# Layer 1: the q and k projections as seven block products each in place of eight, and a PSUM ring of single-bank tiles

## The chip, the cores and the metric

The kernel runs on one core of a Trainium2 chip. The metric is the device time of the whole program in microseconds (us), from launch to end, as the median of several executions. A profiled execution, taken by the hardware profiler, gives the start and length of every instruction; its span runs from the first to the last instruction.

Engines in the profile: PE is the matrix engine (TensorE), with its weight loads listed apart as PEld; DVE is VectorE, ACT is ScalarE, POOL is GpSimd and SP is SyncE, which issues the DMAs here. "L1745" is line 1745 of the kernel.

## The reference, cut to what matters

The input `x` has 128 rows (s) of 256 positions with 256 channels, all in fp32. Two layers follow one another, each with a group normalization, an attention along the 256 positions and a residual. Layer 0 attends with 8 heads, a pair bias and a gate. The change concerns layer 1, a banded attention with 4 heads of 64 channels:

```python
qkv = x2 @ w_in.T + b_in
q, k, v = jnp.split(qkv, 3, axis=-1)
...
scores = jnp.einsum('bhid,bhjd->bhij', q, k) / jnp.sqrt(jnp.asarray(D, x.dtype))
keep = jnp.abs(i - j) <= band          # band = 16
scores = jnp.where(keep, scores, -jnp.inf)
attn = jax.nn.softmax(scores, axis=-1)
out = jnp.einsum('bhij,bhjd->bhid', attn, v)
y = out @ w_out.T + b_out
...
x = x + _L1_conv_ref(_gn(x), L1_conv_w_in, L1_conv_b_in, L1_conv_w_out, L1_conv_b_out, 16)
```

For each row, q and k are the products of a 256 x 256 weight with a 256 x 256 block of activations.

## The kernel before

**Layer 0** fills about two thirds of the time (up to about 2090 us of the span). The change doesn't touch it. A third kernel part, `general_kernel`, runs only if a check at the end finds values out of range, and doesn't run here.

**Layer 1** works on pairs of rows: 64 pairs (`NP`), each an object of class `Pair1`. Activations are kept transposed: `xgT` is [128 partitions, 2 channel halves k, 512], where the 512 columns are the 256 positions of row r = 0 followed by those of row r = 1. The methods of a pair are:

- `turn` (DVE, L1730) transposes the loaded rows; `centre(k)` (ACT, L1735) subtracts the mean, and after k = 1 has POOL add the output bias to the residual (L1737).
- `project("qT" or "kT", m)` (L1745): for each output half m, two matmuls over k, 128 x 128 by 128 x 512, accumulate in one PSUM bank of the ring `ps_mm` (two banks). ACT adds the bias and writes to `qT` or `kT` (L1749).
- `values(r)` (L1760): the v projection of one row, evicted by ACT (L1764).
- `scores(r)` (L1774): small matmuls of 64 x 64 by 64 x 96 into the two banks of `ps_s`; one exponential of both banks on ACT (L1782), and the band mask on POOL (L1784).
- `apply(r)` (L1802): the weighted values into two banks `o_eo` and the softmax sums into `su_eo`, each for odd and even key blocks.
- `combine(r)`: ACT copies the odd sums and outputs (L1812, L1813), DVE adds the even sums (L1814), inverts (L1815), adds the even outputs (L1816) and multiplies (L1818) into `oT`. For the last eight pairs DVE also checks the range of the inverses here (`check`, L958 to L960).
- `out_row(r)` (L1833): the output projection into a bank of `ps_mm`; DVE adds the residual (L1837).

An fp32 `matmul` call shows in the trace as two weight loads and two matmuls, so a pair's projections (8 calls) are 16 matmuls.

The order on each engine is written out by hand in a loop over p with 63 rounds (`manual_schedule`). Three pairs are in flight in a round: `was` (p - 1), `now` (p) and `nxt` (p + 1), with `nn` being prepared. In the first half of a round: `now.scores(0)`, `was.apply(1)`, `was.out_row(0)`, `was.combine(1)`, three of the four projections of `nxt`, `nn.centre(0)`. In the second half: `now.scores(1)`, `now.apply(0)`, `now.combine(0)`, the fourth projection, `nxt.values` for both rows, `was.out_row(1)`, `nn.centre(1)`, `n3.turn()` and, in some rounds, one deferred range check on DVE. An engine takes its instructions in this order, and waits at one whose operands or buffers are not ready.

[...]

Of the kernel before, what the change touches and what calls it, by code (L numbers as in the profile page):

```python
# [21 lines left out]
def bcast(ap, axis, n):  # L22

    ap = ap.unsqueeze(axis)
    shape = list(ap.shape)
    shape[axis] = n
    return ap.broadcast_to(shape)
# [746 lines left out]
def fast_kernel(  # L774
# [889 lines left out]
    rsum1 = dram.tile([NP, H1, 2, I], F32, name="rsum1")  # L1664
    with tc.tile_pool(name="l1", bufs=2) as sb, tc.tile_pool(
        name="l1s", bufs=4
    ) as sm, tc.tile_pool(name="ps1_mm", bufs=2, space=PSUM) as ps_mm, tc.tile_pool(
        name="ps1_s", bufs=1, space=PSUM
    ) as ps_s, tc.tile_pool(name="ps1_o", bufs=1, space=PSUM) as ps_o:

        def mm1(name):
            return ps_mm.tile([P, 512], F32, name=name, tag="mm")

        nM1 = const.tile([P, KC], F32, name="nM1")

        def norm1():

            each = sm.tile([P, 2, C], F32, name="gn_each", bufs=1)
            dev = sm.tile([P, C], F32, name="gn_dev", bufs=1)
            R1c = sm.tile([P, KC], F32, name="gn_R", bufs=1)  # L1680
            ps = ps_s.tile([P, 2, 512], F32, name="ps_gn", tag="s")
            by_group = lambda a: a.rearrange("p (g e) -> p g e", e=GE)
            nc.vector.tensor_copy(by_group(each[:, 0, :]), bcast(st1[:, :, 1], 2, GE))
            nc.tensor.matmul(ps[:, 0, :C], avg, each[:, 0, :], start=True, stop=True)
            nc.vector.tensor_tensor(dev, each[:, 0, :], ps[:, 0, :C], ALU.subtract)
            nc.vector.tensor_mul(dev, dev, dev)
            nc.vector.scalar_tensor_tensor(
                by_group(each[:, 1, :]), bcast(st1[:, :, 2], 2, GE), 1.0 / (S * NB * GE), by_group(dev), ALU.mult, ALU.add
            )
            for n in range(2):  # L1690
                for k in range(KC):
                    nc.tensor.matmul(
                        ps[:, 1, 2 * n + k : 2 * n + k + 1], each[:, n, k * P : (k + 1) * P], avg[:, 0:1],
                        start=True, stop=True,
                    )
            nc.vector.tensor_scalar_add(R1c, ps[:, 1, 2:4], 1e-5)
            nc.gpsimd.tensor_tensor(R1c, R1c, mhalf[:, :KC], ALU.pow)
            nc.vector.tensor_scalar_mul(nM1, ps[:, 1, 0:2], -1.0)
            for n in range(3):
                for k in range(KC):  # L1700
                    at = slice(n * C, (n + 1) * C)
                    nc.vector.tensor_scalar_mul(w_in[:, k, at], w_in[:, k, at], R1c[:, k : k + 1])


        o_eo = [ps_o.tile([P, 2, I], F32, name=f"ps_o1_{n}", tag=f"o{n}") for n in range(2)]
        su_eo = [ps_o.tile([P, I], F32, name=f"ps_su1_{n}", tag=f"su{n}") for n in range(2)]
        for n in range(2):
            nc.vector.memset(o_eo[n], 0.0)
            nc.vector.memset(su_eo[n], 0.0)

        class Pair1:

# [19 lines left out]
            def centre(self, k):  # L1732
                if k == 0:
                    self.xgT = sb.tile([P, KC, N2], F32, name="xgT1", tag="xgT")
                nc.scalar.activation(self.xgT[:, k, :], self.xT[:, k, :], AF.Identity, bias=nM1[:, k : k + 1])  # L1735
                if k == KC - 1:
                    nc.gpsimd.tensor_tensor(self.xt, self.xt, bcast(bout_r, 1, 2 * NB), ALU.add)  # L1737

            def project(self, which, m):
                n = ("qT", "kT").index(which)  # L1740
# [24 lines left out]

            def scores(self, r):

                ps = ps_s.tile([P, 2, 512], F32, name="ps_sc1", tag="s")
                at = lambda q, c, j: ps[:, q, (c * 2 + j) * W : (c * 2 + j + 1) * W]
                for c in range(KC):  # L1770
                    for k in range(NK):
                        for q in range(2):
                            rs = slice(q * D1, (q + 1) * D1)
                            nc.tensor.matmul(  # L1774
                                at(q, c, k // 2)[half(k)],
                                self.kT[rs, c, r * I + k * KB : r * I + (k + 1) * KB],
                                self.qT[rs, c, r * I + q0(k) : r * I + q0(k) + W],
                                start=True, stop=True,
                            )
                e = sm.tile([P, 2, KC, NK // 2 * W], F32, name="e1", tag="e", bufs=3)  # L1780
                ev = e.rearrange("p q c w -> p q (c w)")
                nc.scalar.activation(ev, ps[:, :, : KC * NK // 2 * W], AF.Exp)  # L1782
                for q in range(2):
                    nc.gpsimd.tensor_tensor(  # L1784
                        e[:, q], e[:, q], bcast(bw.rearrange("p b w -> p (b w)"), 1, KC), ALU.mult
                    )
                self.es[r] = e
# [16 lines left out]
                                )  # L1804

            def combine(self, r):

                if r == 0:
                    self.rv = sb.tile([P, 2, I], F32, name="rv1", tag="rv", bufs=3)
                rv = self.rv  # L1810
                odd = sm.tile([P, 3, I], F32, name="odd1", tag="odd", bufs=2)
                nc.scalar.copy(odd[:, 2, :], su_eo[1])  # L1812
                nc.scalar.copy(odd[:, :2, :], o_eo[1])  # L1813
                nc.vector.tensor_tensor(odd[:, 2, :], su_eo[0], odd[:, 2, :], ALU.add)  # L1814
                nc.vector.reciprocal(rv[:, r, :], odd[:, 2, :])  # L1815
                nc.vector.tensor_tensor(odd[:, :2, :], o_eo[0], odd[:, :2, :], ALU.add)  # L1816
                oT = sb.tile([P, 2, I], F32, name="oT1", tag="oT", bufs=3)
                nc.vector.tensor_tensor(oT, odd[:, :2, :], bcast(rv[:, r, :], 1, 2), ALU.mult)  # L1818
                self.oT[r] = oT
                if r == 1 and self.p < NP - LATE:  # L1820
                    nc.sync.dma_start(rsum1[self.p].rearrange("q r i -> q (r i)"), rv[0:P:DH].rearrange("q r i -> q (r i)"))
                elif r == 1 and self.p < NP - 1:
                    check(rv.rearrange("p r i -> p (r i)"), 1e-16, 1e8, sm)
                elif self.p == NP - 1:
                    check(rv[:, r, :], 1e-16, 1e8, sm)

            def out_row(self, r):
                if r == 0:
                    self.yo = sb.tile([P, 2 * NB, C], F32, name="yo", tag="yo")
                ps = mm1("ps_y1")  # L1830
                for b in range(NB):
                    for k in range(KC):
                        nc.tensor.matmul(  # L1833
                            ps[:, b * C : (b + 1) * C], self.oT[r][:, k, b * P : (b + 1) * P], w_out[:, k, :],
                            start=(k == 0), stop=(k == KC - 1),
                        )
                nc.vector.tensor_tensor(  # L1837
                    self.yo[:, r * NB : (r + 1) * NB, :], ps.rearrange("p (b c) -> p b c", b=NB),
                    self.xt[:, r * NB : (r + 1) * NB, :], ALU.add,
                )  # L1840
                s0 = 2 * self.p
                if self.p == NP - 1:
                    nc.sync.dma_start(rows(out, s0 + r, 1), self.yo[:, r * NB : (r + 1) * NB, :])
                elif r == 1:
                    nc.sync.dma_start(rows(out, s0, 2), self.yo)
# [18 lines left out]
        with tc.manual_schedule():  # L1864
# [3 lines left out]
            norm1()  # L1868
            for k in range(KC):
                now.centre(k)  # L1870
            for m in range(KC):
                now.project("qT", m)
                now.project("kT", m)
            for r in range(2):
                now.values(r)
            for k in range(KC):
                nxt.centre(k)
        check_all(eb.rearrange("p h b i -> p (h b i)"), math.exp(-20.0), math.exp(20.0))
        mask_t = sb.tile([S, I], F32, name="mask_all", bufs=1)
        nc.sync.dma_start(mask_t, mask)  # L1880
# [3 lines left out]
        with tc.manual_schedule():  # L1884
            was = Nobody()
            for p in range(NP - 1):
# [6 lines left out]

                now.scores(0)
                was.apply(1)
                was.out_row(0)
                was.combine(1)
                nxt.project("qT", 0)
                nxt.project("kT", 0)
                nxt.project("qT", 1)  # L1900
                nn.centre(0)

                now.scores(1)
                now.apply(0)
                now.combine(0)
                nxt.project("kT", 1)
                if p < NP - 2:
                    nxt.values(0)
                    nxt.values(1)
                was.out_row(1)  # L1910
                nn.centre(1)
                n3.turn()
                if checks and p > 0:
                    checks.pop(0)()
# [88 lines left out]
```

## Time and profile before

| | us |
|---|---|
| median of 3 runs | 3313.72 (3311.55 to 3315.22) |
| the profiled execution, its own time | 3316.03 |
| its span | 3314.3 |
| PE busy in the span | 3157.9 (95%) |
| DVE, POOL, ACT busy | 2121.6, 1962.8, 1452.7 |
| loop of layer 1, 2133.21 to 3280.69: length | 1147.48 |
| PE busy in it | 1147.01 |
| DVE, ACT, POOL busy in it | 672.15, 525.29, 397.41 |

The page lists busy time of each engine, the chain of work that ended last, and the costliest groups of instructions. An engine that is busy in nearly all of a stretch sets its length, as long as its busy time is streaming and not a wait in the middle of an instruction. The mean granted clock of PE is 0.982.

### The profile page before, as it was taken

The page shows a single profiled execution, that of the slowest core. Times are in us where ns is not written, and L with a number is a line of the kernel's source. Part 1 is how long each engine was busy: PE and PEld are TensorE (multiplying, and loading weights), DVE is VectorE, ACT ScalarE, POOL GpSimd, SP SyncE. Part 2 cuts the span into 40 slices and gives each one's busy share as a digit, 9 for nine tenths or more (in the row PEclk, how much of TensorE's full clock was granted, in tenths as well). Part 3 has the DMA queues.
Part 4 walks back from the last instruction along what each step waited for, and adds up shares of the span by engine and source line. Part 5 has one row for each costly group of instructions (what it writes and reads, how often), then busy time and mean ns, then how long its engine had stood idle before and what let it go on. Part 6 is the DMA issues. An engine that isn't in the chain of part 4 may idle for free.

```text
span 3314.3 us, 80768 instructions
## 1 busy us (share of the span) xinstructions
PE 3157.9 (95%) x34656; PEld 1977.2 (60%) x34656; DVE 2121.6 (64%) x3179; ACT 1452.7 (44%) x2121; POOL 1962.8 (59%) x1375
## 2 busy tenths in 40 slices
PE   5389999999999999999999999699999999999998
PEld 3255555555555555555555555466666666666666
DVE  7955666666666666666666666466655555555566
ACT  2264444444444444444444444244444444444443
POOL 2378777777787777787887776233333333333332
PEclk8699999999999999999999999899999999999999
DMA  9951212212221222222122211533333434343431
GB/s 354 375 137 43 75 49 75 75 46 65 72 75 49 75 75 60 64 64 69 49 75 75 75 49 52 104 79 91 85 90 86 92 85 91 85 92 84 92 90 54
DMA packets 464879, 295.92 MB, mean 89 GB/s; under 512 B 312480, under 2 KB 413728, under 8 KB 463360
## 3 DMA queue, kind: packets, MB, share of 16 engines
q1 hardware_dynamic: 459440, 287.76, 31.7%
q8 instruction: 275, 4.51, 0.6%
q10 hardware_dynamic: 5072, 2.90, 0.3%
q14 instruction: 92, 0.75, 0.1%
HBM read 221.85 MB, written 68.75 MB: 88 GB/s over the span
## 4 chain that ended last, share of the span: by engine, by line
PE 91%; DVE 3%; DMA 3%; ACT 1%; POOL 1%; SPq 1%; issue 0%; ACTq 0%; POOLq 0%; DVEq 0%
PE ps_p L1296 21%; PE ps_p L1745 14%; PE ps_sc L1330 8%; PE ps_y L1833 7%; PE ps_ov L1362 7%; PE ps_v L1760 7%; PE ps_y L1417 7%; PE ps_v L1311 6%; PE ps_o L1802 3%; PE ps_su L1370 3%; PE ps_sc L1774 3%; PE ps_x L1274 2%; PE ps_su L1802 1%; DVE st L1178 1%; DVE zst L1103 1%; DMA zt<-in_z_dram 1%
## 5 line engine op out<-in xcount | busy, mean ns | idle before, releaser
L1351 POOL TENSOR_TENSOR eboth<-e 128x512 f32<-128x512 f32 x512 | 640.6, 1273 | 392.9 <-DVE e L1346 389.7
L1346 DVE TENSOR_TENSOR e<-ps_sc,eb 128x1024 f32<-128x1024 f32 x512 | 603.1, 1219 | 307.0 <-ACT ps_sc L1337 306.9
L1337 ACT ACTIVATE ps_sc<-ps_sc 128x1024 f32<-128x1024 f32 x512 | 492.8, 1006 | 509.2 <-PE ps_sc L1330 509.2
L1784 POOL TENSOR_TENSOR e<-e,bw 128x384 f32<-128x384 f32 x256 | 259.5, 1035 | 769.8 <-ACT e L1782 769.8
L1745 PE MATMUL ps_p<-xgT,w_in 128*128 128x512 f32 x1024 | 470.3, 602 | 4.5 <-issue 3.7
L1745 PEld LDWEIGHTS ps_p<-xgT,w_in 128*128 128x128 f32 x1024 | 190.1, 191 | 203.7 <-issue 174.8
L1330 PE MATMUL ps_sc<-qT,kT 32*128 32x256 f32 x4096 | 293.3, 400 | 2.1 <-ACT kT L1300 2.1
L1296 PE MATMUL ps_p<-xnT,wq 128*128 128x512 f32 x512 | 267.3, 634 | 3.5 <-POOL xnT L1283 3.1
L1833 PE MATMUL ps_y<-w_out,oT 128*128 128x256 f32 x1024 | 250.3, 388 | 2.6 <-DVE oT L1818 2.6
L1837 DVE TENSOR_TENSOR yo<-ps_y,xt 128x512 f32<-128x512 f32 x128 | 88.4, 690 | 251.9 <-PE ps_y L1833 149.7
L1362 PE MATMUL ps_ov<-e,v 128*32 128x256 f32 x4096 | 247.7, 382 | 0.0
L1417 PE MATMUL ps_y<-wo,oT 128*128 128x256 f32 x1024 | 242.1, 379 | 2.0 <-POOL oT L1407 1.2
L1417 PEld LDWEIGHTS ps_y<-wo,oT 128*128 128x128 f32 x1024 | 194.3, 190 | 82.5 <-issue 59.3
L1311 PE MATMUL ps_v<-wv,xnT 128*128 128x256 f32 x1024 | 242.2, 379 | 0.0
L1330 PEld LDWEIGHTS ps_sc<-qT,kT 32*128 32x128 f32 x4096 | 184.9, 184 | 94.4 <-issue 83.6
L1296 PE MATMUL ps_p<-xnT,wk 128*128 128x512 f32 x512 | 240.8, 592 | 0.0
L1296 PE MATMUL ps_p<-xgT,wg 128*128 128x512 f32 x512 | 236.8, 605 | 0.0
L1760 PE MATMUL ps_v<-w_in,xgT 128*128 128x256 f32 x1024 | 231.8, 379 | 0.0
L1815 DVE RECIPROCAL rv<-odd 128x256 f32<-128x256 f32 x128 | 224.4, 1753 | 4.4
L1760 PEld LDWEIGHTS ps_v<-w_in,xgT 128*128 128x128 f32 x1024 | 194.4, 190 | 53.5 <-issue 30.1
L1317 DVE TENSOR_TENSOR v<-ps_v,vb_r 128x512 f32<-128x512 f32 x128 | 88.6, 692 | 206.8 <-PE ps_v L1311 206.8
L1311 PEld LDWEIGHTS ps_v<-wv,xnT 128*128 128x128 f32 x1024 | 189.6, 190 | 50.8 <-issue 31.0
(169 smaller groups left out, 4989.9 us busy)
## 6 DMA issues: line engine op xcount, KB each, us to landing
xa<-in_x_dram SPq DMA_DIRECT2D x8, 4096.0 KB
xt<-in_x_dram SPq DMA_DIRECT2D x64, 512.0 KB
x<-xo SPq DMA_DIRECT2D x16, 2048.0 KB
xs<-x SPq DMA_DIRECT2D x256, 128.0 KB
xt<-x SPq DMA_DIRECT2D x64, 512.0 KB
rvb<-rsum SPq DMA_DIRECT2D x252, 128.0 KB
out_dram<-yo SPq DMA_DIRECT2D x63, 512.0 KB
zt<-in_z_dram SPq DMA_DIRECT2D x15, 2048.0 KB
```

The source lines that it names most:

```text
L1296: nc.tensor.matmul(ps, w[:, k, m * P : (m + 1) * P], getattr(self, src)[:, k, :], start=(k == 0), stop=(k == KC - 1),)
L1311: nc.tensor.matmul(self.ps_v[:, b * C : (b + 1) * C], self.xnT[:, k, t * P : (t + 1) * P], wv[:, k, :], start=(k == 0), stop=(k == KC - 1),)
L1330: nc.tensor.matmul(self.pss[q // 2][:, q % 2, b, :], self.kT[rs, c, r * I + b * P : r * I + (b + 1) * P], self.qT[rs, c, r * I : (r + 1) * I],
L1337: nc.scalar.activation(self.pss[a], self.pss[a], AF.Exp)
L1346: nc.vector.tensor_tensor(e, pss[a], eb[:, h : h + 2], ALU.mult)
L1351: nc.gpsimd.tensor_tensor(t, es[a][:, :, 0, :], es[a][:, :, 1, :], ALU.add)
L1362: nc.tensor.matmul(ov[q * D0 : (q + 1) * D0, c, :], self.v[:, r, b, h * D0 : (h + 1) * D0], es[q // 2][:, q % 2, b, :], start=(b == 0), st ...
L1417: nc.tensor.matmul(self.ps_y[:, b * C : (b + 1) * C], self.oT[r][:, k, b * P : (b + 1) * P], wo[:, k, :], start=(k == 0), stop=(k == KC - 1),)
L1745: nc.tensor.matmul(ps, w_in[:, k, n * C + m * P : n * C + (m + 1) * P], self.xgT[:, k, :], start=(k == 0), stop=(k == KC - 1),)
L1760: nc.tensor.matmul(ps[:, b * C : (b + 1) * C], self.xgT[:, k, t * P : (t + 1) * P], w_in[:, k, 2 * C : 3 * C], start=(k == 0), stop=(k == ...
L1784: nc.gpsimd.tensor_tensor(e[:, q], e[:, q], bcast(bw.rearrange("p b w -> p (b w)"), 1, KC), ALU.mult)
L1833: nc.tensor.matmul(ps[:, b * C : (b + 1) * C], self.oT[r][:, k, b * P : (b + 1) * P], w_out[:, k, :], start=(k == 0), stop=(k == KC - 1),)
```

## The change

The 2 x 2 block product of a weight (blocks by k and m) with the activations of a pair (blocks by k and by row r) has eight block products of 128 x 128 by 128 x 256. The change forms it from seven, in a variant of Strassen's form, for q (n = 0) and for k (n = 1):

- `mix_weights` makes four sums of weight blocks (`wst`) once, on POOL. `differences` makes four sums of activation blocks (`dT`, 256 columns each) for each pair, on POOL.
- `product(n, i)` is one block product. Two PSUM tiles hold a matrix: in `x` the products 1, 6, 7 and 4 accumulate one on another, and after each ACT copies the partial sum out (with a bias) before the next may add to it. In `y` product 2, then 5, then 3 are placed; `join(n, i)` on DVE adds a saved partial sum to `y` and writes a block of `qT` or `kT`.
- The rings `ps_mm` and `ps_s` become one ring of four single-bank tiles, used by the scores (two tiles), the products (two for each matrix) and the values (one each). The exponential of `scores` becomes two instructions, one for each tile.
- `out_row` has no ring any more: it writes to the free halves of the two banks that hold the softmax sums (`su_y`).
- `combine` is cut in three (`copy_odd`, `invert`, `weigh`), which the first half of a round places among the products. All products and joins of a pair stand in the first half of a round now; the second half has none.

```diff
-    ) as sm, tc.tile_pool(name="ps1_mm", bufs=2, space=PSUM) as ps_mm, tc.tile_pool(
-        name="ps1_s", bufs=1, space=PSUM
-    ) as ps_s, tc.tile_pool(name="ps1_o", bufs=1, space=PSUM) as ps_o:
+    ) as sm, tc.tile_pool(name="ps1_s", bufs=4, space=PSUM) as ps_s, tc.tile_pool(
+        name="ps1_o", bufs=1, space=PSUM
+    ) as ps_o:
 
         def mm1(name):
-            return ps_mm.tile([P, 512], F32, name=name, tag="mm")
+            return ps_s.tile([P, 512], F32, name=name, tag="s")
 
         nM1 = const.tile([P, KC], F32, name="nM1")
+        wst = sb.tile([P, 4, 2, P], F32, name="wst", bufs=1)
...
+        def mix_weights():
+
+            a = [[w_in[:, k, 0 : 2 * C].rearrange("p (n m c) -> p m n c", n=2, m=KC)[:, m] for k in range(KC)]
+                 for m in range(KC)]
+            s1, s2, s3, s4 = (wst[:, n] for n in range(4))
+            nc.gpsimd.tensor_tensor(s1, a[1][0], a[1][1], ALU.add)
+            nc.gpsimd.tensor_tensor(s2, s1, a[0][0], ALU.subtract)
+            nc.gpsimd.tensor_tensor(s3, a[0][0], a[1][0], ALU.subtract)
+            nc.gpsimd.tensor_tensor(s4, a[0][1], s2, ALU.subtract)
+
         o_eo = [ps_o.tile([P, 2, I], F32, name=f"ps_o1_{n}", tag=f"o{n}") for n in range(2)]
-        su_eo = [ps_o.tile([P, I], F32, name=f"ps_su1_{n}", tag=f"su{n}") for n in range(2)]
+        su_y = ps_o.tile([P, 2, 2, I], F32, name="ps_su_y1", tag="su")
+        su_eo = [su_y[:, n, 0] for n in range(2)]
...
+            def differences(self):
+
+                self.dT = sb.tile([P, 4, I], F32, name="dT1", tag="dT")
+                b = [[self.xgT[:, k, r * I : (r + 1) * I] for r in range(2)] for k in range(KC)]
+                t1, t2, t3, t4 = (self.dT[:, n] for n in range(4))
+                nc.gpsimd.tensor_tensor(t1, b[0][1], b[0][0], ALU.subtract)
+                nc.gpsimd.tensor_tensor(t2, b[1][1], t1, ALU.subtract)
+                nc.gpsimd.tensor_tensor(t3, b[1][1], b[0][1], ALU.subtract)
+                nc.gpsimd.tensor_tensor(t4, b[1][0], t2, ALU.subtract)
...
+            def product(self, n, i):
+
+                if len(self.ps) == n:
+                    self.ps.append([mm1("ps_qk") for _ in range(2)])
+                x, y = (ps[:, :I] for ps in self.ps[n])
...
+                to, lhs, rhs, start = {
+                    1: (x, w(0, 0), b(0, 0), True),
+                    2: (y, w(0, 1), b(1, 0), True),
+                    6: (x, wst[:, 1, n], self.dT[:, 1], False),
+                    5: (y, wst[:, 0, n], self.dT[:, 0], True),
+                    7: (x, wst[:, 2, n], self.dT[:, 2], False),
+                    4: (x, w(1, 1), self.dT[:, 3], False),
+                    3: (y, wst[:, 3, n], b(1, 1), False),
+                }[i]
+                nc.tensor.matmul(to, lhs, rhs, start=start, stop=True, skip_group_check=True)
...
+                if i in (1, 6, 7):
+                    at = (1, 6, 7).index(i)
+                    nc.scalar.activation(u[:, at], x, AF.Identity, bias=bias(at // 2))
+                elif i == 4:
+                    nc.scalar.activation(self.to[n][:, 1, 0:I], x, AF.Identity, bias=bias(1))
+
+            def join(self, n, i):
+                m, r, at = {2: (0, 0, 0), 5: (1, 1, 2), 3: (0, 1, 1)}[i]
+                nc.vector.tensor_tensor(
+                    self.to[n][:, m, r * I : (r + 1) * I], self.ps[n][1][:, :I], self.u[n][:, at], ALU.add
+                )
...
-                nc.scalar.activation(ev, ps[:, :, : KC * NK // 2 * W], AF.Exp)
+                for q in range(2):
+                    nc.scalar.activation(ev[:, q], ps[q][:, : KC * NK // 2 * W], AF.Exp)
...
-                ps = mm1("ps_y1")
+                ps = su_y[:, :, 1]
...
                 now.scores(0)
                 was.apply(1)
+                nxt.begin_fast()
+                nxt.product(0, 1)
+                was.copy_odd(1)
+                nxt.product(1, 1)
+                for n in range(2):
+                    nxt.product(n, 2)
+                    nxt.join(n, 2)
+                was.invert(1)
+                for i in (6, 5, 7):
+                    for n in range(2):
+                        nxt.product(n, i)
+                for n in range(2):
+                    nxt.join(n, 5)
+                was.weigh(1)
                 was.out_row(0)
-                was.combine(1)
-                nxt.project("qT", 0)
-                nxt.project("kT", 0)
-                nxt.project("qT", 1)
+                for n in range(2):
+                    nxt.product(n, 4)
+                    nxt.product(n, 3)
+                    nxt.join(n, 3)
                 nn.centre(0)
 
                 now.scores(1)
                 now.apply(0)
                 now.combine(0)
-                nxt.project("kT", 1)
                 if p < NP - 2:
                     nxt.values(0)
                     nxt.values(1)
                 was.out_row(1)
                 nn.centre(1)
+                nn.differences()
                 n3.turn()
```

## The prediction

> **What bounds the kernel now.** I read the sums over windows first, because the change touches only the loop of layer 1 and a share over the whole span would mix stages; then the timeline of each engine over one round of that loop; then one place where PE really waits, to price a wait. The two halves of one round, busy time by engine:
>
> ```profile
> core 0: us, PE busy (x) PEld busy (x) DVE busy (x) ACT busy (x) POOL busy (x), PEclk, DMA share, GB/s
> 2404.91:2414.10 9.19, 9.19 (x150) 5.57 (x149) 5.85 (x7) 3.05 (x5) 1.96 (x2) 1.00 0.76 173
> 2414.10:2423.30 9.20, 9.20 (x157) 7.08 (x156) 4.32 (x4) 5.34 (x9) 4.28 (x3) 1.00 0.02 4
> ```
>
> PE is busy for all of 18.39 us; DVE, ACT and POOL have 8 to 12 us of slack, the DMA share doesn't bind. So a matmul taken away is time taken away, unless PE begins to wait. PE's own timeline of the round shows the price of each stage:
>
> ```profile
> 2404.91 0.89 PE L1774 MATMUL ps_sc<-qT,kT 64*64 64x96 f32 x32
> 2407.02 1.99 PE L1833 MATMUL ps_y<-w_out,oT 128*128 128x256 f32 x8
> 2408.85 5.31 PE L1745 MATMUL ps_p<-xgT,w_in 128*128 128x512 f32 x12
> 2414.10 0.89 PE L1774 MATMUL ps_sc<-qT,kT 64*64 64x96 f32 x32
> 2416.21 1.98 PE L1745 MATMUL ps_p<-xgT,w_in 128*128 128x512 f32 x4
> 2418.03 3.62 PE L1760 MATMUL ps_v<-w_in,xgT 128*128 128x256 f32 x16
> 2421.48 1.89 PE L1833 MATMUL ps_y<-w_out,oT 128*128 128x256 f32 x8
> ```
>
> From start to start, 16 matmuls of 256 columns take 2421.48 - 2418.03 = 3.45 us, 0.2156 each, with a new weight load each time. In the weight loads of the projection the step is 0.429 for 512 columns:
>
> ```profile
> 2409.28 0.19 PEld L1745 LDWEIGHTS ps_p<-xgT,w_in 128*128 128x128 f32 x1 [0.24 <-issue]
> 2409.71 0.19 PEld L1745 LDWEIGHTS ps_p<-xgT,w_in 128*128 128x128 f32 x1 [0.24 <-issue]
> ```
>
> A single 256-column matmul lasts 0.379 (the rows of L1760), so a reader on ACT or DVE can start 0.42 after the last pass of a product starts: ACT begins at 2410.77, 0.04 after the modelled end (2410.14 + 0.59) of the projection that it evicts.
>
> **What the Trainium skill says.** "TensorE: Matmul & The Clock Gate", section "LDWEIGHTS (loading the stationary operand)": a load takes columns / 1.2 ns, 107 for 128. The trace agrees in the place where PE waits (below): the second load starts 0.11 us after the first. "PSUM — Partial Sum Buffer", section "PSUM bank collisions raise a hardware error": engines must be kept apart by bank, not by address, so a product may not enter a bank that ACT or DVE still reads; the trace before has no bank that is read and then added to, so the chain of products 1, 6, 7, 4 is new. Its section "The four PSUM rules" allows a synchronised read of a partial sum amid an accumulation; no run shows it yet. "SBUF — State Buffer", section "Who interferes with whom": a DVE instruction with one SBUF input doesn't contend with POOL, one with two does. The trace agrees: L1816 (PSUM and SBUF) takes 0.63 at 2418.85 beside POOL's L1737, while L1818 (two SBUF inputs) right after it takes 1.59 in place of 0.69.
>
> **The change, part by part.** Times t count from the first matmul of a round (2404.91).
>
> Removed: 16 matmuls x 0.429 = 6.864. Added: 14 products x 2 passes x 0.2156 = 6.037. Net -0.83 a round, x 63 rounds = -52 us. The switches between 64-row and 128-row matmuls stay four a round.
>
> The wait that ends this. The place where PE waits in before:
>
> ```profile
> 1842.96 2.50 POOL L1283 TENSOR_TENSOR xnT<-xgT,rs_r 128x512 f32<-128x512 f32 x2 [0.55 <-DMA rs_r<-rs_d]
> 1844.29 2.35 PE L1296 MATMUL ps_p<-xnT,wq 128*128 128x512 f32 x4 [0.34 <-POOL xnT L1283]
> 1844.29 0.30 PEld L1296 LDWEIGHTS ps_p<-xnT,wq 128*128 128x128 f32 x2 [0.74 <-POOL xnT L1283]
> ```
>
> The first POOL multiply ends at 1844.24; the load starts 0.05 later; the loads stand 0.11 apart, so columns stream 0.16 after the releaser's end. A release that comes before the preceding matmul starts costs nothing, since the load runs under it.
>
> Now ACT and DVE in the first half:
>
> ```profile
> 2405.95 0.81 ACT L1782 ACTIVATE e<-ps_sc 128x768 f32<-128x768 f32 x1 [1.45 <-PE ps_sc L1774]
> 2407.16 0.37 ACT L1812 COPY odd<-ps_su 128x256 f32<-128x256 f32 x1 [0.40 <-PE ps_su L1802]
> 2407.43 0.59 ACT L1813 COPY odd<-ps_o 128x512 f32<-128x512 f32 x1
> 2409.72 0.41 DVE L1814 TENSOR_TENSOR odd<-ps_su,odd 128x256 f32<-128x256 f32 x1
> 2410.17 1.75 DVE L1815 RECIPROCAL rv<-odd 128x256 f32<-128x256 f32 x1
> 2411.84 0.63 DVE L1816 TENSOR_TENSOR odd<-ps_o,odd 128x512 f32<-128x512 f32 x1
> ```
>
> Starts show that the engines overlap neighbours: ACT steps 0.27 for the 256 copy, 0.49 for the 512 copy (2421.68 to 2422.17 after L1764), and 0.59 for a biased 512 eviction of 0.69 (2414.20 to 2414.79). Less 0.22 for 256 columns (L1813's 0.59 less L1812's 0.37), my estimate for a biased 256 eviction is a step of 0.37 and a length of 0.47. For a join I take L1814: 0.42, step 0.34.
>
> Product (0,1) streams at 2.22, where the output row streamed, its second pass at 2.43. ACT: eviction from 2.43 + 0.42 = 2.85, then the two copies of `copy_odd` from 3.22 and 3.49, then the eviction of (1,1) from 3.98 to 4.45. PE goes on through (1,1), (0,2), (1,2), (0,6), and would start (1,6) at 4.37; that one waits for the eviction: 4.45 + 0.16 = 4.61. **A stall of 0.24.** Its bounds: none, if the eviction steps only as a copy does (0.27); 0.4, if ACT doesn't overlap neighbours.
>
> DVE goes on from there: join (1,2) 4.49, the sum 4.83, reciprocal 5.28 to 6.95; join (0,5) waits for ACT's copy of product 7 (PE 6.12, ACT 6.54 to 7.01) and runs at 7.04, join (1,5) at 7.47, `weigh` 7.81 and 8.47, the residual of the output row 9.08, join (0,3) 9.69 to 10.11. Products 5 and 3, the output row at 6.77 to 8.49, and products 4 find their releases early. PE ends its products at 10.22 and, with the switch, wants scores(1) at 10.31. The second score tile takes over the bank of `y` for q, so it needs join (0,3): 10.11, early by 0.16 after the release. No stall, but the slack is that thin; lost, it costs what it is late by: 0 to 0.3.
>
> **Last rounds.** Six rounds (was = 56 to 61) carry a range check after L1818:
>
> ```profile
> 3277.59 0.42 DVE L958 TENSOR_SCALAR chk<-rv 128x512 f32<-128x512 f32 x1
> 3278.05 0.69 DVE L959 SCALAR_TENSOR_TENSOR chk<-rv,chk 128x512 f32<-128x512 f32 x1
> 3278.77 0.69 DVE L960 TENSOR_REDUCE ok<-chk 128x1 f32<-128x512 f32 x1
> ```
>
> Before, nothing on PE waited behind it. Now the residual and join (0,3) do: about 1.67 of steps on DVE, so scores(1) streams 1.5 late, x 6 = +9 us. The checks at the end of other rounds (DVE 2167.67 to 2170.19) put join (0,2) at about 4.35 and join (1,2) at 4.68; product 5 of q and k ask at 4.82 and 5.26 and the chain meets the old one at join (1,5), so 0.
>
> **Edits beside other work.** On ACT eight evictions of 256 columns stand for four of 512, and the exponential comes in two parts (+0.7 us in all); six joins on DVE add 2.1 to 2.5. Both fit into the slack. POOL's four differences: an estimate of 0.70 each, from 0.98 for 384 and 1.27 for 512 columns; they start when `centre(1)` ends at -0.4, so t2, the first that PE wants (product 6 at 3.9), is done at 1.1 and the mask of e moves from 1.93 to about 2.6; it ends at 4.6 and is wanted by `apply(0)` at 11. The first round's differences start at 2135.2 and are as early. `mix_weights` runs once, beside the first projections on POOL, which idles there (14.85 us before L1784). No DMA is added or moved. Output rows without a ring: in a round each finds its residual done (t 0.8 and 9.8). At the very end `now.apply(1)` sums (3298.23) wait for the residual that L1837 ends at 3299.84: +1.6; the larger memset of `su_y` +0.4.
>
> Sum: -52 + 62 x 0.24 (14.9) + 9 + 2 = -26. The profiled execution, 3316.03, becomes 3290; the median of the runs stands 2.3 lower, so **3288 us**.
>
> **Rivals.** *No wait at (1,6)*: ACT copies step faster than I take; for it speaks the 0.27 step of L1812, against it the bias, 0.10 more in L1749 than in L1764. 3313.7 - 52 + 11 = 3273, and 3264 if the late checks hide too.
>
> *The thin slack is lost*: join (0,3) is 0.3 late at scores(1) in each round, by hand-offs with two semaphores (0.05 each). +19: 3307. The six-deep DVE queue ahead speaks for it, the L1814 to L1816 steps against.
>
> *Slower*: hand-offs from ACT or DVE break the weight load's cover. Ten products a round wait for a release into their bank (6, 7, 4, 5, 3 of q and k). If each streams 0.16 late, as at 1844.29, that is 1.6 against 0.83. It decides from about four, with the 11 us of the ends counted; at seven, 63 x (1.12 - 0.83) + 11 = +29: 3343. Against it: the load at 2410.14 carries a wait for DVE that had been met, and keeps the 0.43 step.
>
> **How the numbers follow.** A difference under 0.2% (6.6 us) can't be told from none. Forecast (3278 to 3298) 0.52; no wait (3262 to 3278) 0.20; slack lost (3298 to 3320) 0.17; slower 0.11. Of the third, 0.05 falls within 3307 to 3320, so faster 0.84, same 0.05, slower 0.11. The range 3266 to 3307 leaves out 0.03 below, and 0.05 and 0.11 above.
>
> **What would show it.** Right: a round of about 17.8 us with one PE gap, before the second product 6, released by ACT; gaps of 1.5 before scores(1) in the six late rounds, released by DVE's join. Wrong: gaps before products 5, 7, 4 or 3, or before scores(1) in every round; 256-column steps over 0.216; DVE's joins longer than 0.42.

## The result, and the profile after

| | before | after |
|---|---|---|
| median of four runs each, us | 3312.64 (3310.42 to 3315.22) | 3291.18 (3289.32 to 3293.29) |
| ratio, 95% interval | | 0.9935 (0.9918 to 0.9952) |
| span of the profiled execution | 3314.3 | 3291.6 |
| loop, from its first scores to those of the last pair (63 rounds) | 1151.1 | 1125.6 |
| a normal round | 18.39 | 17.80 |

The kernel is 21 us faster; the forecast was 26 faster, 3288. The loop alone gives 25.5. The rest lies outside it: in the profile after, the loop begins 1.4 later, behind layer 0, and what follows the last scores takes 31.3 in place of 30.0. Less these two, 25.5 is the 22.7 between the two spans. Both vary from run to run: in the other runs below the loop begins between 2128.9 and 2143.3 (2133.2 before), and the part after the last scores takes 31.2 to 33.6.

First the round, in the view of sums over windows (one row for each half of the round that starts at 2406.01; columns: window, its length, busy time and instructions of each engine, clock, DMA) and PE's timeline of the same round in the kernel after, without the rows of `apply`:

```profile
core 0: us, PE busy (x) PEld busy (x) DVE busy (x) ACT busy (x) POOL busy (x), PEclk, DMA share, GB/s
2406.01:2416.32 10.31, 10.31 (x166) 8.52 (x165) 7.84 (x12) 5.14 (x12) 3.74 (x5) 1.00 0.67 155
2416.32:2423.81 7.49, 7.49 (x154) 6.33 (x153) 4.13 (x5) 4.29 (x9) 5.69 (x5) 1.00 0.01 2
```

```profile
2406.01 0.89 PE L1835 MATMUL ps_sc<-qT,kT 64*64 64x96 f32 x32
...
2408.12 1.99 PE L1785 MATMUL ps_qk<-xgT,w_in 128*128 128x256 f32 x8
2409.95 2.99 PE L1785 MATMUL ps_qk<-dT,wst 128*128 128x256 f32 x12
2412.77 1.89 PE L1904 MATMUL ps_su_y<-w_out,oT 128*128 128x256 f32 x8
...
2415.79 0.59 PE L1785 MATMUL ps_qk<-xgT,wst 128*128 128x256 f32 x2
2416.32 0.89 PE L1835 MATMUL ps_sc<-qT,kT 64*64 64x96 f32 x32
```

All products of q and k stand in the first half, which is now 10.31 long, and the second has 7.49. The eight matmuls from 2408.12 take 1.83, from start to start, as did the output row that stood at this place before (2407.02 to 2408.85). But the group of twelve takes 2.82, where twelve steps of 0.2156 are 2.59: 0.23 more. PE is counted as busy in it all the same. The weight loads show the hole (timeline of PEld, the same round, and the view of waits from 2400 to 3100, whose columns are total, times and longest):

```profile
2409.73 0.41 PEld L1785 LDWEIGHTS ps_qk<-dT,wst 128*128 128x128 f32 x2
2410.51 0.51 PEld L1785 LDWEIGHTS ps_qk<-dT,wst 128*128 128x128 f32 x3 [0.37 <-ACT u L1790]
```

```profile
PEld ps_qk L1785 <- ACT u L1790: 14.3, 39, 0.4
```

The load of the second product 6 waits for ACT's copy of a partial sum, once in each of 39 rounds: 0.37 of the loader's time, of which 0.23 reaches the matmuls. It is the only wait of PE in that stretch that an engine ends. Three more lines of that round are needed below: DVE's join of q's product 3, the last thing that scores(1) wants, and POOL's first difference and masks:

```profile
2415.74 0.41 DVE L1796 TENSOR_TENSOR qT<-ps_qk,u 128x256 f32<-128x256 f32 x1
```

```profile
2404.31 1.18 POOL L1756 TENSOR_TENSOR dT<-xgT 128x256 f32<-128x256 f32 x1
2407.80 1.95 POOL L1846 TENSOR_TENSOR e<-e,bw 128x384 f32<-128x384 f32 x2
```

**Rounds that are not normal.** Rounds are counted from 0, and round 0 takes 14.2 in both kernels. Rounds 2 to 9 and 11 to 14, twelve in all, take 18.46; rounds 57 to 61 take 18.00, 18.00, 18.66, 18.33 and 18.00; the last one, without values, takes 15.54 where before it took 14.94. Before, all the others took 18.39. What sets the twelve apart is a range check on DVE, three instructions over 512 columns that the end of the round before has issued. (Round 10 has one over 256 columns and stays at 17.80.) DVE's timeline in such a round (it starts at 2185.14), and POOL's masks beside it, in the kernel after; then DVE and POOL in a round of before with such a check (start 2165.80):

```profile
2187.01 1.21 DVE L958 TENSOR_SCALAR chk<-eb 128x512 f32<-128x512 f32 x1
2188.25 1.37 DVE L959 SCALAR_TENSOR_TENSOR chk<-eb,chk 128x512 f32<-128x512 f32 x1
2189.66 0.69 DVE L960 TENSOR_REDUCE ok<-chk 128x1 f32<-128x512 f32 x1
2190.26 0.41 DVE L1796 TENSOR_TENSOR qT<-ps_qk,u 128x256 f32<-128x256 f32 x1
```

```profile
2186.93 2.14 POOL L1846 TENSOR_TENSOR e<-e,bw 128x384 f32<-128x384 f32 x2
```

```profile
2167.67 0.39 DVE L958 TENSOR_SCALAR chk<-eb 128x512 f32<-128x512 f32 x1
```

```profile
2167.72 2.60 POOL L1784 TENSOR_TENSOR e<-e,bw 128x384 f32<-128x384 f32 x2 [4.68 <-ACT e L1782]
```

After, POOL starts 0.08 before L958, and L958 takes 1.21; before, it starts 0.05 after it, and L958 takes 0.39 (means over eight such rounds: 1205 and 384 ns). L959 takes 1.37 in the one and 1.38 in the other. The first join, 2190.26, is then 5.1 into the round, and PE waits for it:

```profile
2190.73 1.99 PE L1785 MATMUL ps_qk<-dT,wst 128*128 128x256 f32 x8 [0.39 <-DVE qT L1796]
```

**The late rounds**, in the kernel after (PE's, ACT's, then DVE's timeline, round 57):

```profile
3164.06 1.09 PE L1835 MATMUL ps_sc<-qT,kT 64*64 64x96 f32 x32
```

```profile
3163.73 0.48 ACT L1792 ACTIVATE kT<-ps_qk,bin_c 128x256 f32<-128x256 f32 x1 [0.39 <-PE ps_qk L1785]
```

```profile
3164.06 0.69 DVE L960 TENSOR_REDUCE ok<-chk 128x1 f32<-128x512 f32 x1
3164.67 0.68 DVE L1908 TENSOR_TENSOR yo<-ps_su_y,xt 128x512 f32<-128x512 f32 x1
3165.26 0.41 DVE L1796 TENSOR_TENSOR qT<-ps_qk,u 128x256 f32<-128x256 f32 x1
```

The join of q's product 3 does run late, 1.2 after the scores began, but the scores don't wait for it: PE has only 0.2 in it (1.09 in place of 0.89). In these rounds the pool gave scores(1) the banks of `x` of q and `x` of k: the waits written on the instructions are for ACT twice, where rounds 0 to 56 have one for ACT and one for DVE. ACT reads `x` of k last, until 3164.21, and the second tile of the scores starts 0.20 late. Why the pool chose otherwise in these rounds was not tried.

### The profile page after: what moved, and what is told of

Read it like the earlier page. It is cut to its first block, busy times and chain, and to the rows that moved or that the text cites. A ratio compares the mean times of both kernels' runs of the same rounds, so it can differ in the third digit from the quotient of the medians.

```text
span 3291.6 us, 83426 instructions
## 1 busy us (share of the span) xinstructions
PE 3128.1 (95%) x35412; PEld 2116.9 (64%) x35412; DVE 2244.0 (68%) x3556; ACT 1517.9 (46%) x2501; POOL 2159.8 (66%) x1631
## 4 chain that ended last, share of the span: by engine, by line
PE 89%; DVE 5%; DMA 2%; issue 2%; ACT 1%; POOL 1%; ACTq 0%; DVEq 0%; POOLq 0%; SPq 0%
PE ps_p L1296 22%; PE ps_qk L1785 11%; PE ps_sc L1330 8%; PE ps_v L1821 7%; PE ps_ov L1362 7%; PE ps_su_y L1904 7%; PE ps_v L1311 7%; PE ps_y L1417 7%; PE ps_su L1370 3%; PE ps_o L1864 3%; PE ps_sc L1835 3%; PE ps_x L1274 2%; DVE st L1178 1%; PE ps_su_y L1864 1%; DVE zst L1103 1%
## 5 line engine op out<-in xcount | busy, mean ns | idle before, releaser
L1904 PE MATMUL ps_su_y<-w_out,oT 128*128 128x256 f32 x1024 | 243.7, 381 | 4.2 <-DVE odd L1882 2.8
L1790 ACT ACTIVATE u<-ps_qk,bin_c 128x256 f32<-128x256 f32 x378 | 178.2, 479 | 140.7 <-PE ps_qk L1785 132.9
L1904 PEld LDWEIGHTS ps_su_y<-w_out,oT 128*128 128x128 f32 x1024 | 195.2, 191 | 31.9 <-DVE odd L1882 3.5
L1785 PE MATMUL ps_qk<-dT,wst 128*128 128x256 f32 x756 | 191.6, 389 | 5.1 <-DVE qT L1796 5.1
```

Of the source, the lines that this page charges most:

```text
L1785: nc.tensor.matmul(to, lhs, rhs, start=start, stop=True, skip_group_check=True)
L1904: nc.tensor.matmul(ps[:, b], self.oT[r][:, k, b * P : (b + 1) * P], w_out[:, k, :], start=(k == 0), stop=(k == KC - 1),)
```

## The experiments

Ten runs follow, in three groups, each group on a chip of its own with runs of the kernel before beside it (its medians: 3313.7, 3321.4, 3320.8): mask_order to eight_products, then fixed_ring to best, then best2 with changed_again, the changed kernel unedited. The ratio to before is what compares between groups; within the profile, the loop (the row of that name in the table of the result) leaves layer 0 out. A round "with early check" is one of the twelve.

| run | median, us | ratio to before, 95% | loop | rounds: normal, with early check, late |
|---|---|---|---|---|
| after | 3291.18 | 0.9935 (0.9918 to 0.9952) | 1125.6 | 17.80, 18.46, 18.0 to 18.7 |
| mask_order | 3282.60 | 0.9904 (0.9889 to 0.9920) | 1116.5 | 17.80, 17.80, 18.0 |
| check_moved | 3280.73 | 0.9906 (0.9890 to 0.9921) | 1116.6 | 17.80, 17.80, 18.0 to 18.1 |
| copy_late | 3276.94 | 0.9891 (0.9876 to 0.9906) | 1114.7 | 17.57, 18.46, 17.8 to 18.7 |
| eight_products | 3317.88 | 1.0012 (1.0006 to 1.0019) | 1152.3 | 18.40, 18.40, 18.4 |
| fixed_ring | 3311.38 | 0.9963 (0.9949 to 0.9976) | 1134.9 | 17.80, 18.46, 19.5 to 20.2 |
| both | 3278.18 | 0.9868 (0.9853 to 0.9883) | 1104.7 | 17.57, 17.75, 17.8 to 17.9 |
| both_moved | 3279.15 | 0.9873 (0.9858 to 0.9888) | 1102.8 | 17.57, 17.57, 17.8 |
| best | 3274.99 | 0.9857 (0.9842 to 0.9873) | 1103.3 | 17.57, 17.57, 17.6 to 19.7 |
| best2 | 3278.05 | 0.9869 (0.9854 to 0.9884) | 1101.6 | 17.57, 17.57, 17.6 to 17.7 |
| changed_again | 3301.08 | 0.9939 (0.9925 to 0.9952) | 1125.3 | 17.80, 18.46, 18.0 to 18.7 |

### Why does a check cost 0.66? mask_order and check_moved

```diff
-                for q in range(2):
+                for q in (1, 0):
                     nc.gpsimd.tensor_tensor(
                         e[:, q], e[:, q], bcast(bw.rearrange("p b w -> p (b w)"), 1, KC), ALU.mult
```

> Edit: in scores, POOL masks the half q = 1 of e before the half q = 0; nothing else. Theory (shared port): in the 13 rounds with a check at their end, POOL's first mask (start t 1.79) takes the SBUF port that it shares with DVE just before the check's L958 (t 1.87), which then lasts 1.14 to 1.21 us in place of 0.38. With q = 1 first the first mask can start only when the second exponential is done, about t 1.92, after L958: L958 back to 0.38 to 0.39, these rounds from 18.46 to 17.80, the normal ones stay at 17.80; 13 x 0.66 = 8.6 us less than the changed kernel, about 3282.5. Rival (the check's own length and place in the DVE queue make the late join (0,2)): L958 may get shorter but the rounds stay at 18.4 and more, 3291. Slower side: the second mask, now q = 0, ends no earlier and apply needs it only at t 11, so no loss in either theory.

Only the order of two POOL instructions changes. DVE's and POOL's timelines of the same round (start 2181.95), POOL's from its last difference on:

```profile
2183.82 0.50 DVE L958 TENSOR_SCALAR chk<-eb 128x512 f32<-128x512 f32 x1
2184.36 1.37 DVE L959 SCALAR_TENSOR_TENSOR chk<-eb,chk 128x512 f32<-128x512 f32 x1
```

```profile
2183.30 0.74 POOL L1759 TENSOR_TENSOR dT<-xgT,dT 128x256 f32<-128x256 f32 x1
2184.00 2.59 POOL L1846 TENSOR_TENSOR e<-e,bw 128x384 f32<-128x384 f32 x2
```

L958 starts before the masks again, and the round is 17.80. The loop is 9.2 shorter, against 8.6 expected, 0.3 of it in round 0; the late rounds with a check of the sums come down from 18.66 and 18.33 to 18.0 too. The check's three instructions and their place are the same, so their bare length isn't what costs here.

L958 takes 0.50, though, where 0.38 to 0.39 was expected: POOL's last difference is still running when it starts, until 2184.04, and L958 ends 0.28 after that. In the kernel after, the first mask lasts 1.00, until 2187.93, and L958 ends 0.29 later. So what L958 loses is the rest of the POOL instruction that it finds running.

The second edit, check_moved, takes the check from the end of the round to a place before `combine(0)`:

```diff
+                if checks and p > 0:
+                    checks.pop(0)()
                 now.combine(0)
...
                 n3.turn()
-                if checks and p > 0:
-                    checks.pop(0)()
```

> Edit: the deferred range check is issued between now.apply(0) and now.combine(0) in place of the end of the round, where DVE waits for PE and ACT about from t 10.8 to 12.5; nothing else. If the check in front of join (0,2) is what costs 0.66 in 13 rounds (either by the port or by its length): these rounds 17.80, 8.6 us less than the changed kernel, about 3282.5. If the cost is of another origin (for example the transposes or transfers of those rounds), 3291 and 18.46 stay. If the check collides with the join of the sums in combine(0) in its new place, up to 0.5 a round for nothing on PE, since apply(1) comes 9 us later: no loss expected.

```profile
2189.27 0.42 DVE L958 TENSOR_SCALAR chk<-eb 128x512 f32<-128x512 f32 x1
2189.72 0.69 DVE L959 SCALAR_TENSOR_TENSOR chk<-eb,chk 128x512 f32<-128x512 f32 x1
```

Here (DVE's timeline, 10.8 into a round) the check runs where DVE has nothing that a product waits for, and finds no POOL instruction running. Its rounds take 17.80 and the loop is 9.0 shorter: a second edit, another means, the same 9 us. Both together say: the cost was a slow L958 in front of join (0,2).

### Why does PE wait at the second product 6? copy_late

```diff
-                was.copy_odd(1)
                 nxt.product(1, 1)
+                was.copy_odd(1)
```

> Edit: was.copy_odd(1) (two ACT copies) is issued after nxt.product(1,1) in place of before it, so that ACT evicts product (1,1) directly after (0,1). Theory: the 0.23 us that PE waits before the second product 6 is the two copies ahead of the eviction in ACT's queue. Then (1,1) is evicted by about t 3.7, PE doesn't wait there, join (1,2) comes earlier, and a normal round takes 17.57: about 49 x 0.23 = 11 us less than the changed kernel, 3280. The reciprocal needs the copies, which end at about 4.5 in place of 4.0: DVE reaches it at 5.27 anyway, so no new wait. Rival (the wait has its origin in the accumulation itself, in PE turning from one bank to another or in the copy of a partial sum): 17.80 stays, 3291. A second rival: the time is taken back before scores(1), as PE wants it 0.23 earlier (10.08) while join (0,3) still ends at 10.15: 0.1 to 0.15 of the gain is lost in each round, 3285 to 3288.

PE's timeline of a normal round (start 2400.50):

```profile
2404.44 2.75 PE L1785 MATMUL ps_qk<-dT,wst 128*128 128x256 f32 x12
2407.03 1.89 PE L1904 MATMUL ps_su_y<-w_out,oT 128*128 128x256 f32 x8
```

Start to start, the twelve now take 2.59, which is 12 x 0.2156, and a normal round is 17.57, 0.23 shorter (round 10, with its narrower check, stays at 17.80): the whole 0.23 was the copies in ACT's queue, and the row for PEld and L1785 is gone from the waits of 2400 to 3100. The rival that expected the slack of 0.16 before scores(1) to be eaten is wrong: the joins of product 2 move up as well. The rounds with a check stay at 18.46, bound by DVE.

### Do the other parts of the change give anything? eight_products

```diff
-                nxt.begin_fast()
-                nxt.product(0, 1)
+                nxt.project("qT", 0)
                 was.copy_odd(1)
...
-                for i in (6, 5, 7):
-                    for n in range(2):
-                        nxt.product(n, i)
-                for n in range(2):
-                    nxt.join(n, 5)
+                nxt.project("qT", 1)
                 was.weigh(1)
                 was.out_row(0)
...
+                nxt.project("kT", 1)
                 nn.centre(0)
```

> Edit: q and k by the old eight-product project calls (qT 0, kT 0, qT 1, kT 1, all four in the first half at the places of the products); differences and mix_weights are left out; the ring of four single-bank tiles, the exponential in two parts, the output rows without a ring and combine in three stay. Theory: the gain is the matmul time of the seven products alone, the rest brings nothing: round 18.4 (17.80 + 0.83 - 0.23), total within 3 us of the kernel before, 3311 to 3316. Rival: the single-bank ring or the output rows give part of the gain: under 3305. Other rival: the rest costs (the check rounds lose 0.66 here too, or the combine in parts makes PE wait): 3318 to 3325. By the port theory POOL's mask is early here too and L958 lasts about 1.2, but no join waits behind it, so PE loses nothing.

The round is 18.40 as before, and the total 0.12% above before (interval 0.06% to 0.19%): 3317.9, above the 3311 to 3316 that were expected. So the ring of single-bank tiles, the exponential in two parts and the output rows without a ring gain no time of their own. The loop is 1.2 longer than before, and 1.0 of that is the last round, 15.93 for 14.94, where PE waits for `combine` before an output row:

```profile
3283.70 1.99 PE L1904 MATMUL ps_su_y<-w_out,oT 128*128 128x256 f32 x8 [0.92 <-DVE odd L1882]
```

L958 is slow here also: POOL's mask starts 0.3 before it, and it takes 981 ns on the mean of eight. But no round with a check is longer, since no join stands behind it.

### Why are the late rounds cheap? fixed_ring

```diff
-    ) as sm, tc.tile_pool(name="ps1_s", bufs=4, space=PSUM) as ps_s, tc.tile_pool(
+    ) as sm, tc.tile_pool(name="ps1_s", bufs=1, space=PSUM) as ps_s, tc.tile_pool(
...
+        turns = []
+
         def mm1(name):
-            return ps_s.tile([P, 512], F32, name=name, tag="s")
+            turns.append(name)
+            return ps_s.tile([P, 512], F32, name=name, tag=f"s{len(turns) % 4}")
```

> Edit: the four PSUM tiles of the ring get names of their own and are handed out in strict turn, in place of by the pool's choice; nothing else. In all rounds, the six late ones too, scores(1) then takes the banks of x and of y for q, where the pool of the changed kernel gave it x of q and x of k in the late rounds. Theory (the bank decides what a late join (0,3) costs): the six late rounds take about 17.8 + 1.5 = 19.3 us in place of 18.0 to 18.7, as the prediction had worked out for them, so about +6 us over the changed kernel, 3297; all other rounds as before (17.80, and 18.46 with a check at their end). Rival (the late rounds are cheap since the join isn't late, or since PE waits elsewhere anyway): late rounds stay at 18.0 to 18.7 and the time at 3291.

The late rounds take 19.47 (20.17 and 19.82 where a check of the sums comes on top), and the loop is 9.3 longer than after. The theory gave 19.3. Against a normal round of 17.80 the bank costs 1.67, where the prediction had 1.5; against the late rounds of the kernel after, which lose 0.2 anyhow, it is 1.47 to 1.51 in each of six, the last one included. PE's timeline of round 57 (lines of this kernel are 3 higher):

```profile
3172.82 0.38 PE L1838 MATMUL ps_sc<-qT,kT 64*64 64x96 f32 x2
3174.49 0.89 PE L1838 MATMUL ps_sc<-qT,kT 64*64 64x96 f32 x30 [1.30 <-DVE qT L1799]
```

The second tile of the scores starts 1.67 after the first. That is the gap that the prediction had worked out, 0.17 longer. It is real wherever the ring hands out y of q, and the pool's choice of the bank avoided it in the changed kernel.

### The edits together: both, both_moved, best, best2

`both` joins mask_order and copy_late, `both_moved` joins check_moved and copy_late.

> Edit: the two single edits together, POOL's masks with q = 1 first and copy_odd after product (1,1). If the causes are separate (port in the rounds with a check, ACT's queue in all): every normal round 17.57 and every round with a check 17.57 to 17.65, since L958 takes 0.38 to 0.50 and join (0,2) is there before product 5 asks; 3292 - 8.6 - 11 - 3 (13 x 0.23) = 3269 to 3271. If the check's own length is the limit once the other wait is gone, its 13 rounds stay above 17.8: 3274.

> Edit: the range check between apply(0) and combine(0), and copy_odd after product (1,1). All rounds but the late six 17.57 (PE busy throughout, 18.39 - 0.83 = 17.56 by the matmuls alone): 3291 - 8.6 - 14 = 3268 to 3270. Below that nothing is left in the round but matmuls. If it is above 3274, something of the two edits collides (the check with the sum in combine).

Loops of 1104.7 and 1102.8. In `both` a round with a check takes 17.75, 0.18 more than a normal one: with ACT's copy no longer in the way, the check's length, L958's 0.49 included, begins to show, and the load of product 5 waits 0.3 for the join in each of the twelve. Moved away it costs nothing (17.57). The expected totals, 3268 to 3274, were for the first chip; by the ratios the two stand at 0.987, where 3268 to 3274 is 0.986 to 0.988.

`best` also moves the late range checks out of `weigh`:

```diff
-                    check(rv.rearrange("p r i -> p (r i)"), 1e-16, 1e8, sm)
+                    late.append(rv.rearrange("p r i -> p (r i)"))
...
                 now.apply(0)
+                if late:
+                    check(late.pop(), 1e-16, 1e8, sm)
                 if checks and p > 0:
...
```

> Edit: as the one before, and the range checks of the inverses of the last pairs also stand between apply(0) and combine(0) in place of within weigh. If the late rounds' excess (0.2 to 1.1 each, about 2 to 2.5 us in all) comes from these checks ahead of the joins on DVE: all late rounds 17.57, so 2 us less than without this edit, 3266 to 3268. If not, the same time.

The late rounds come down to 17.57 but for one of 19.69. In round 58 the sums have just been loaded, and two checks stand before `combine(0)` (DVE's timeline, then POOL's and PE's):

```profile
3169.20 1.00 DVE L958 TENSOR_SCALAR chk<-sums 128x512 f32<-128x512 f32 x1 [0.50 <-DMA sums<-rsum]
3170.24 2.73 DVE L959 SCALAR_TENSOR_TENSOR chk<-sums,chk 128x512 f32<-128x512 f32 x1
```

```profile
3169.88 2.54 POOL L1749 TENSOR_TENSOR xt<-xt,bout_r 128x1024 f32<-128x1024 f32 x1
```

```profile
3174.07 1.99 PE L1904 MATMUL ps_su_y<-w_out,oT 128*128 128x256 f32 x8 [1.85 <-DVE odd L1882]
```

The output row shares its bank with the sums and waits until `combine` has read them. L959 is so long because it found POOL's add running: it ends 0.55 after it. This edit gave back what it gained. `best2` takes no deferred check in that round.

> The changed kernel itself, unedited, to stand on the same chip as the next kernel: rounds of 17.80, 18.46 and 18.0 again, ratio to before 0.9935 as measured.

> Edit: as the kernel labelled best, and no deferred check is taken in round 58, in which its operand has only just been loaded (there DVE waited for that transfer, its next instruction took 2.73 us, and PE waited 1.85 us for the sum in combine to free the bank of su_y). Expected: round 58 at 17.57 in place of 19.69, all rounds at 17.57 to 17.7, and the loop 62 x 17.57 + 13.96 less the short last round: about 2 us less than best. Against the changed kernel on the same chip: 8.6 (checks) + 14.3 (62 x 0.23 at the second product 6) + 2.1 (late rounds) = 25 us less. Rival: the transfer's wait only moves to the next round: 19.7 there, no gain over best.

Beside the changed kernel on the same chip it is 23.0 us faster (3278.05 to 3301.08), its loop 23.8; expected were 25. The 0.23 came in all 62 rounds, and 0.66 more in each of the twelve; what is short is 0.8 of the late rounds, for which too much was counted, and 0.3 in round 0. The four combined kernels can't be told apart by their ratios (0.9857 to 0.9873, intervals overlapping), and only best's interval lies apart from that of copy_late; all of them lie below the interval of after. By the loop, best2 is the shortest: 1101.6.

## Why the prediction was right, and where two steps were wrong

- **Removed and added matmuls, -0.83 a round**: shown. With the wait taken away a round is 17.57, 0.82 below 18.39, and with eight products in the new frame it is 18.40.
- **The stall of 0.24 at the second product 6**: shown, 0.23, by the trace and by copy_late, with the queue order on ACT as the cause. It is the largest cost of the change as it stands. The account of DVE's queue behind it held too: the joins (1,2), (0,5) and (1,5) were put at 4.49, 7.04 and 7.47 and ran at 4.48, 7.04 and 7.47.
- **The slack at scores(1)**: held. The join of q's product 3 ends at 10.15 in the round (10.11 predicted) and scores(1) starts at 10.31 without a wait. The rival that lost it fell.
- **"Ten products wait for a release"**, the slower case: fell. Only one load shows such a wait in a normal round; a hand-off that comes early costs nothing, as at the load that the prediction cited. The Trainium skill ("PSUM — Partial Sum Buffer", "The four PSUM rules") allows a synchronised read amid an accumulation; the traces agree, with no time beyond the ordinary wait (copy_late: 12 x 0.2156).
- **"+1.5 each = +9" in the last rounds**: wrong in the changed kernel. The step that failed is "The second score tile takes over the bank of `y` for q". That holds in rounds 0 to 56; in the late ones the pool gave x of k. Measured: 0.2 in a late round, for ACT's release of that bank. With the bank forced the price is 1.67 over a normal round, near the 1.5.
- **"The checks at the end of other rounds ... so 0"**: wrong, +0.66 in each of the twelve early rounds and in round 59, +0.33 in round 60 with its smaller operand, 8.9 in all. The failed step lies one paragraph further on: "the mask of e moves from 1.93 to about 2.6". It was 1.79. The first difference needs only what `centre(0)` wrote, so it ran at -1.7, before `centre(1)` ended, and three instead of four stood in front of the mask; and the first half of the exponential was ready sooner. So POOL came 0.08 before L958 in place of after it. Where L958 takes 0.50 (mask_order), joins (0,2) and (1,2) run at 4.4 and 4.8, near the predicted 4.35 and 4.68, and cost nothing; in the twelve rounds PE waits before product 5, a gap that the prediction had listed among the signs of being wrong. The prediction had also quoted half of the rule in the Trainium skill, "SBUF — State Buffer", "Who interferes with whom". The section excepts DVE's two-port modes, counts `tensor_scalar` among the operations that can enter them, and says that whoever issues first keeps the shared ports while the other waits. L958 is such a `tensor_scalar`, and the trace agrees: 0.39 when it starts first, and 1.21, to 0.29 after the mask's end, when POOL does. That it truly ran in such a mode no run shows; that the order of the two decides, mask_order does.
- **"Output rows without a ring: in a round each finds its residual done", epilogue +1.6**: right for the residual in normal rounds. But the bank has the sums in it as well, and in the last round, where no values stand between, the output row waited about 1 us for `combine` to read them (0.92 of idle PE, the same as in eight_products): 15.54, where 17.80 less the 3.45 of the values is 14.35, and 0.2 is the late check. The end after the last scores took 1.3 more, but the executions of the other kernels spread over 2.4, so the 1.6 is neither shown nor refuted.

Summed over the loop: 61 rounds x -0.592, +0.6 in the last, +7.9 early checks, +2.0 late rounds over 17.80 (five times 0.2, 0.66, 0.33) = -25.6; measured -25.5. The forecast's part for the loop was -52 + 14.9 + 9 = -28. It came out so near because some 8 us too much in the late rounds (9 against six times 0.2) stood against 9 too little in the rounds with checks. That the two cancelled is luck; the -0.83 and the stall are not. Had only one of the two steps failed, the time would have lain some 8 or 9 us from the forecast, still inside its range.

## What to carry to other kernels

When work moves earlier on DVE or POOL, look at which instruction of the other it now starts just ahead of: a shift of 0.14 us made one DVE instruction three times as long, and it counted only because a hand-off to the bottleneck stood behind it. Before a partial sum is read and then added to, put the reader first in its engine's queue; two copies that nobody was waiting for yet were 0.23 of the 0.83 us that a round could gain. What a late reader costs depends on whose buffer comes next in the ring, so read the waits of the last rounds separately and don't extend the steady state to them.

## What the runs showed of the hardware that was not expected

- A DVE instruction from SBUF to SBUF with one input (L958, 128x512) took 384 ns where it started 0.05 before a POOL multiply, and 1205 ns where it started 0.08 after one. What it loses is the rest of the POOL instruction that runs when it starts: in all 95 such cases in the traces of these runs, with lengths from 0.48 to 1.21, it ended 0.28 to 0.29 after that instruction's end. POOL's next instruction, which in the kernel after starts 0.87 after L958, adds nothing.
- With two inputs (L959, 128x512) the same holds with 0.55, in all 108 such cases: 1.37 in the kernels before and after, and the 2.73 of round 58 of best, behind an add of 2.54. Where none was running it took 0.69. So the order of starts to the tenth of a microsecond, and the length of the instruction ahead, set how long these DVE instructions last.
- Adding a product to a bank whose partial sum ACT has just copied costs no more than the wait: in copy_late, with the copies early enough, the twelve matmuls of products 6, 5 and 7 keep the 0.2156 step.
